# Layer 0 without a branch, with folded weights and word masks: one change to a two-layer graph attention kernel

## The chip, the cores and the metric

The kernel runs on one core of a Trainium2 chip. The metric is the time of one execution on the device in microseconds (us), median of several executions. In what follows PE is the tensor engine, PEld its weight loads, DVE the vector engine, ACT the scalar engine, POOL the GpSimd engine and SP the engine that issues most loads. The granted clock is the share of its full speed that PE was given. The chain of waits is the work that ended last, followed back step by step to what released it. A seam is a stretch between two stages in which PE has next to nothing to do. PSUM is where these kernels keep the tiles that PE writes.

## The reference, cut to what matters

There are 4096 nodes with 512 features, a dense 4096x4096 adjacency of edge weights, and 32 graphs of 128 nodes each, so that one row tile of 128 rows is one graph.

```python
# layer 0: attention inside each graph, softmax over the whole row
h = relu(layernorm(x))
q, k, v = h @ Wq.T + bq, h @ Wk.T + bk, h @ Wv.T + bv
a = where(same_graph, q @ k.T / sqrt(512), 0)
scores = (a + adj + adj) * where(same_graph, 1, -1e6)
x = x + (softmax(scores) * same_graph) @ v
# layer 1: graph attention with 8 heads of 64 columns; the term of row i cancels in its softmax
h = relu(layernorm(x))
mx = h @ W ;  t[j, head] = sum_d mx[j, head, d] * a_dst[head, d]
x = x + softmax over {j : adj[i, j] > 0} of t[j], applied to mx
```

Outside its own graph a row's scores are -2e6 times an edge weight. They are 0 for a missing edge, and so they count in the softmax's sum.

## The kernel before, where the change touches it

A flag from the group pointers decides at the start whether layer 0 runs in its tiled form. Layer 0 goes through 16 groups of two row tiles, in plain order. The buffers of x come from the same pool of three as the adjacency's.

```python
graphs_in_tiles = nc.values_load(flag_i[0:1, 0:1], min_val=0, max_val=1)
with tc.If(graphs_in_tiles > 0) as branch:
    with (tc.tile_pool(name="adj0", bufs=3) as ap, tc.tile_pool(name="sb0", bufs=2) as sb, ...):
        for g in range(NT // G):
            xg = load_x(ap, G * g, G)
            qT, kT, v = projections(sb, ps_t, ps_p, wq, wk, wv, xg)   # norm, transposes, q, k, v
            for t in range(G):
                i = G * g + t
                a = ap.tile([P, N], F32, name="a")
                nc.sync.dma_start(a, adj[ts(i, P), :])
                mask_T(ps_a, sb, a, i)        # a > 0 in bf16, 32 transposes, cast to bytes, store
                ...                           # graph-id matmul, scores, s = own block's scores
                for n, (c0, c1) in enumerate(others):
                    nc.vector.tensor_reduce(least[:, n : n + 1], a[:, c0:c1], AX.X, ALU.min)
                ...                           # nmax = -(largest score of the row)
                for n, (c0, c1) in enumerate(others):
                    nc.scalar.activation(a[:, c0:c1], a[:, c0:c1], AF.Exp, bias=nmax,
                                         scale=2.0 * NEG, accum_out=sums[:, n : n + 1])
                ...                           # exp of s, transpose, times v
                nc.vector.scalar_tensor_tensor(x1, po, rsum, xg[:, t, :], ALU.mult, ALU.add)
                nc.scalar.dma_start(x1_d[i], x1)
```

Layer 1 first prepares 32 tiles (norm, transposes, product with W, t on VectorE, exp, split in two parts) and then aggregates: for each row tile 32 x 3 matmuls of 348 columns over the transposed mask.

```python
ta = sb.tile([P, H, HD], F32, name="ta")
nc.vector.tensor_mul(ta.rearrange("p h d -> p (h d)"), pm, a_sb)
nc.vector.tensor_reduce(t, ta, AX.X, ALU.add)
```

## Time and profile before

The median is 1378.01 us in the comparison with the changed kernel (1377.6 to 1379.15, 4 runs). The stages of the profiled execution, read from the stage boundaries that the prediction shows further down:

| stage | from, to (us) | length |
|---|---|---|
| start, until layer 0's loads have landed | 0 to 30 | 30 |
| layer 0 | 30 to 712 | 682 |
| layer 1, preparation with its two seams | 712 to 878 | 166 |
| layer 1, aggregation | 878 to 1369 | 491 |
| tail | 1369 to 1378.5 | 9.5 |

To compare versions of layer 0, I use the **group spacing**: the time between the first group's last output and the last group's, divided by 15. Here it is (713.97 - 77.02)/15 = 42.5 us. In the changed order the last of the 15 is short, because the last group has no next group to prepare.

In the groups of instructions (line, engine, operation, tile, shapes, count, then busy us and mean ns of one, then the idle time before them), these two are what VectorE does to an adjacency tile besides the mask's cast:

```profile
L243 DVE TENSOR_REDUCE least<-a 128x1 f32<-128x3968 f32 (+30 forms) x62 | 138.6, 2277 | 1.8 <-DMA a<-adj 1.8
L141 DVE TENSOR_SCALAR a<-a 128x2048 bf16<-128x2048 f32 x64 | 77.3, 1221 | 6.8 <-DMA a<-adj 6.8
```

The minimum costs 138.6/32 = 4.3 us a tile.

### The profile page before, as it was taken

How to read it: one execution, taken by the hardware profiler on the slowest of the kernel's cores; microseconds unless marked ns; L12 is line 12 of the kernel's file. 1: busy time of each engine (PE TensorE's matmuls, PEld its weight loads, DVE VectorE, ACT ScalarE, POOL GpSimd, SP SyncE). 2: the span in 40 equal slices, each digit the busy share in tenths (PEclk: the TensorE clock that was granted, in tenths of full speed). 3: DMA queues.
4: the chain of work that ended last, by engine and by line, in shares of the span. 5: the costliest groups of instructions: out<-in, count | busy, mean ns of one | idle time of the engine just before them, and what ended most of it. 6: DMA issues, size and time to landing. Idle time of an engine off the chain costs nothing.

```text
span 1378.5 us, 15799 instructions
## 1 busy us (share of the span) xinstructions
PE 1189.4 (86%) x6313; PEld 961.9 (70%) x6313; DVE 642.0 (47%) x1194; ACT 463.4 (34%) x606; POOL 166.4 (12%) x264
## 2 busy tenths in 40 slices
PE   2897888897878977788848999799999999999997
PEld 1665555665556655565624444699999999999997
DVE  3856756656656566474538888121112111211121
ACT  0334544334444244433522233232223222322230
POOL 0101010100001000000004554010001000100010
PEclk9988988988889887898869999899999999999999
DMA  6245442344532344223222221212111211121110
GB/s 254 113 160 183 183 151 110 121 168 184 183 134 102 132 183 183 105 95 152 108 90 65 56 67 39 92 62 87 67 62 61 90 64 62 61 92 62 61 31 33
DMA packets 39527, 148.50 MB, mean 108 GB/s; under 512 B 4368, under 2 KB 4368, under 8 KB 35344
## 3 DMA queue, kind: packets, MB, share of 16 engines
q1 hardware_dynamic: 25616, 113.80, 23.6%
q10 hardware_dynamic: 9216, 16.78, 3.2%
q0 software_dynamic: 4608, 16.78, 3.0%
q8 instruction: 52, 0.85, 0.3%
q14 instruction: 35, 0.29, 0.1%
HBM read 113.79 MB, written 33.55 MB: 107 GB/s over the span
## 4 chain that ended last, share of the span: by engine, by line
PE 44%; DVE 5%; ACT 2%; POOL 2%; issue 1%; DMA 1%; SPq 0%; ACTq 0%; POOLq 0%; DVEq 0%
PE pg L424 36%; PE pm L388 4%; PE pp L179 2%; PE pp L190 1%; DVE e L404 1%; DVE hn L130 1%; DVE ta L390 1%; ACT parts L411 1%; POOL rstd L128 1%; PE pp L269 1%; ACT hT L134 1%; ACT a L253 1%; DMA row<-x_d 1%; POOL parts L412 0%; DVE at L150 0%
## 5 line engine op out<-in xcount | busy, mean ns | idle before, releaser
L424 PE MATMUL pg<-parts,at 128*128 128x348 f32 x3072 | 491.3, 323 | 9.1 <-ACT at L420 9.1
L424 PEld LDWEIGHTS pg<-parts,at 128*128 128x128 f32 x3072 | 491.0, 189 | 9.7 <-ACT at L420 9.7
L431 DVE TENSOR_TENSOR tot<-tot,pg 128x522 f32<-128x522 f32 x32 | 22.4, 700 | 412.4 <-ACT tot L430 412.4
L430 ACT COPY tot<-pg 128x522 f32<-128x522 f32 x32 | 19.1, 596 | 363.5 <-PE pg L424 363.5
L243 DVE TENSOR_REDUCE least<-a 128x1 f32<-128x3968 f32 (+30 forms) x62 | 138.6, 2277 | 1.8 <-DMA a<-adj 1.8
L253 ACT ACTIVATE a<-a,nmax 128x3968 f32<-128x3968 f32 (+30 forms) x62 | 123.7, 1996 | 22.3 <-DVE nmax L247 21.2
L145 PE MATMUL pa<-ident_b,a 128*128 128x128 bf16 x1024 | 88.9, 241 | 45.7 <-DVE a L141 22.8
L388 PE MATMUL pm<-w_sb,hT 128*128 128x512 f32 x256 | 116.7, 609 | 11.3 <-ACT hT L134 11.3
L179 PE MATMUL pp<-hT,wq 128*128 128x256 f32 x512 | 121.7, 399 | 5.2 <-ACT hT L134 4.8
L145 PEld LDWEIGHTS <-a 128*128 128x128 bf16 x1024 | 75.6, 109 | 63.4 <-issue 33.0
L420 ACT CAST at<-at 128x4096 fp32r<-128x4096 fp8e4 x32 | 115.9, 3621 | 5.3 <-DMA row<-x_d 4.9
L179 PEld LDWEIGHTS pp<-hT,wq 128*128 128x128 f32 x512 | 101.2, 201 | 23.2 <-ACT hT L134 9.0
L179 PE MATMUL pp<-hT,wk 128*128 128x256 f32 x512 | 113.1, 379 | 0.0
L190 PE MATMUL pp<-wv,hT 128*128 128x512 f32 x256 | 112.5, 593 | 0.0
L148 ACT ACTIVATE at<-pa 128x1024 fp8e4<-128x1024 bf16 x64 | 64.9, 1017 | 140.0 <-PE pa L145 140.0
L179 PEld LDWEIGHTS pp<-hT,wk 128*128 128x128 f32 x512 | 97.4, 190 | 13.1
L480 POOL TENSOR_TENSOR tot<-tot,row 128x512 f32<-128x512 f32 x32 | 41.3, 1290 | 462.9 <-DVE tot L447 462.9
L388 PEld LDWEIGHTS pm<-w_sb,hT 128*128 128x128 f32 x256 | 48.2, 194 | 69.9 <-issue 51.3
L193 DVE TENSOR_TENSOR v<-pp,bv_sb 128x512 f32<-128x512 f32 x32 | 22.1, 692 | 147.6 <-PE pp L190 147.6
L190 PEld LDWEIGHTS pp<-wv,hT 128*128 128x128 f32 x256 | 48.7, 190 | 54.3 <-issue 53.5
L269 PE MATMUL pp<-v,sT 128*128 128x512 f32 x64 | 64.8, 1117 | 24.7 <-ACT sT L267 24.6
L150 DVE CAST at<-pa 128x1024 fp8e4<-128x1024 bf16 x64 | 78.0, 1219 | 5.6 <-PE pa L145 4.0
(79 smaller groups left out, 958.1 us busy)
## 6 DMA issues: line engine op xcount, KB each, us to landing
a<-adj SPq DMA_DIRECT2D x32, 2048.0 KB, 9.1
at_d<-at POOLq DMA_DIRECT2D x32, 512.0 KB, 3.9
row<-x_d SPq DMA_DIRECT2D x64, 256.0 KB, 3.2
at<-at_d SPq DMA_DIRECT2D x32, 512.0 KB, 4.5
xg<-x SPq DMA_DIRECT2D x16, 512.0 KB, 7.1
x_d<-x ACTq DMA_DIRECT2D x32, 256.0 KB, 6.5
out<-tot ACTq DMA_DIRECT2D x32, 256.0 KB, 3.7
wq<-wqT SPq DMA_DIRECT2D x1, 1024.0 KB, 5.2
```

Source lines behind the costliest of these rows:

```text
L145: nc.tensor.transpose(pa[:, c, :], a01[:, ts(8 * q + c, P)], ident_b)
L148: nc.scalar.activation(dst, pa, AF.Copy, saturate=False)
L150: nc.vector.tensor_copy(dst, pa, saturate=False)
L179: nc.tensor.matmul(pp[:, : G * P], w[:, k, ts(m, P)], hT[:, k, :], start=(k == 0), stop=(k == KC - 1),)
L190: nc.tensor.matmul(pp, hT[:, k, ts(t, P)], wv[:, k, :], start=(k == 0), stop=(k == KC - 1))
L243: nc.vector.tensor_reduce(least[:, n : n + 1], a[:, c0:c1], AX.X, ALU.min)
L253: nc.scalar.activation(a[:, c0:c1], a[:, c0:c1], AF.Exp, bias=nmax, scale=2.0 * NEG, accum_out=sums[:, n : n + 1],)
L269: nc.tensor.matmul(po, sT, v[:, t, :], start=True, stop=True)
L388: nc.tensor.matmul(pm, hT[:, k, :], w_sb[:, k, :], start=(k == 0), stop=(k == KC - 1))
L420: nc.scalar.copy(at, at8)
L424: nc.tensor.matmul(pg[:, c, : 2 * CW1], at[:, j, :], parts[:, j, c].rearrange("p s w -> p (s w)"), start=(j == 0), stop=(j == NT - 1),)
L480: nc.gpsimd.tensor_add(num, num, row)
```

## The change

The intent has six parts:

- Layer 0 runs unconditionally for the case of one graph per tile. The bounds and the pointers are checked once at the end, and one branch there leads to a general path.
- q.k is formed as (h M + c).h with M = Wq.T Wk folded at the start, so that one projection takes the place of two.
- The exponentials run without the row maximum; the final check covers the range.
- Four mask bytes are packed in a 32-bit word. PE transposes 8 words per tile instead of 32 bf16 blocks.
- The next group's norm, projection and values are written among the present group's work.
- In layer 1, t comes out of PE as extra columns of the weights.

```diff
-    with tc.If(graphs_in_tiles > 0) as branch:
+    def mask_bytes(pool, a):
+        a8 = pool.tile([P, N], FP8, name="a8")
+        nc.vector.tensor_scalar(
+            a8.rearrange("p (c w b) -> p c b w", c=NW, b=BY),
+            a.rearrange("p (c b w) -> p c b w", c=NW, b=BY),
+            0.0, 1.0, ALU.is_gt, ALU.add, saturate=False,
+        )
...                                     (8 transposes of a8.bitcast(F32) per tile, two copies)
-            for g in range(NT // G):
-                xg = load_x(ap, G * g, G)
-                qT, kT, v = projections(sb, ps_t, ps_p, wq, wk, wv, xg)
+        xg[0] = load_x(sb, 0, G)
+        m_sb, c_sb, u_sb, z_sb = fold(wp, ps_t, ps_p)
...                                     (loads, and the first group's norm, values, projection)
+        for g in range(NG):
+            last = g + 1 == NG
+            if not last:
+                nhT, nr = normed(g + 1)
+            ss = []
+            for t in range(G):
+                i = G * g + t
+                a8 = mask_bytes(sb, aa[i])
+                ss.append(soften(aa[i], hT, gT, r, t, i))
+                mask_T(ps_a, sb, a8, i)
+                if i + G < NT:
+                    aa[i + G] = load_adj(ap, i + G)
+            if not last:
+                ngT = queries(nhT)
+            nvs = []
+            for t in range(G):
+                attend(ss[t], vs[t], g, t)
+                if not last:
+                    nvs.append(values(nhT, t))
+            if g + 2 < NG:
+                xg[g + 2] = load_x(sb, G * (g + 2), G)
...                                     (in soften: no minimum, no maximum, no graph-id matmul)
-        ta = sb.tile([P, H, HD], F32, name="ta")
-        nc.vector.tensor_mul(ta.rearrange("p h d -> p (h d)"), pm, a_sb)
+                pm = project1(ps_m, hT, w1x)      (2 x 260 columns: 256 of W and 4 of t)
...
+    bad = nc.values_load(bad_i[0:1, 0:1], min_val=0, max_val=1)
+    with tc.If(bad > 0):
...                                     (the general path)
```

x moved from the pool with three buffers to the pool `sb`, which has two.

## The prediction

> **What bounds the kernel now.** I first cut the execution at the stage boundaries that the chain of waits shows and read each engine's busy time per stretch. The columns are: stretch, length, busy us (instructions) of PE, weight load, DVE, ACT, POOL, then granted clock, DMA share, GB/s.
>
> ```profile
> 0.00:30.00 30.00, 3.32 (x12) 2.36 (x12) 8.80 (x16) 2.48 (x3) 2.65 (x14) 1.00 0.62 232
> 30.00:712.00 682.00, 557.84 (x2835) 403.15 (x2835) 422.01 (x693) 285.76 (x442) 53.21 (x92) 0.85 0.38 142
> 712.00:724.00 12.00, 3.05 (x7) 1.10 (x7) 2.35 (x6) 0.60 (x1) 0.79 (x2) 0.50 0.65 219
> 724.00:868.00 144.00, 133.46 (x388) 64.30 (x389) 121.81 (x255) 41.95 (x95) 67.24 (x123) 0.98 0.19 54
> 868.00:878.00 10.00, 0.88 (x4) 0.49 (x3) 0.56 (x3) 4.65 (x4) 1.23 (x1) 0.70 0.63 209
> 878.00:1369.00 491.00, 490.82 (x3072) 490.54 (x3071) 83.80 (x217) 127.51 (x63) 40.02 (x31) 1.00 0.20 64
> ```
>
> The reader is to see three kinds of time. The last stage (layer 1's aggregation, 491 us) has PE busy all the time at full clock: only fewer or shorter matmuls would move it. Layer 0 (682 us for 16 groups of two row tiles, so 42 us a group) has PE at 82% with the clock at 0.85. And 52 us (0 to 30, 712 to 724, 868 to 878) are seams where PE does next to nothing.
>
> Next I took one group of layer 0 from the chain of waits (start, us, what).
>
> ```profile
> 632.86 14.13 PE pp L179 x64
> 646.99 6.87 PE pp L190 x16
> 653.86 0.91 PE pss L230 x8
> ...
> 660.60 1.90 PE pa L145 x16
> ...
> 670.82 2.07 PE pp L269 x2
> 672.89 1.25 PE pt L133 x6
> 674.17 0.60 ACT hT L134
> 674.82 14.08 PE pp L179 x64
> ```
>
> The period is 674.82 - 632.86 = 42.0 us. 21 us of it is dense projection, the other 21 us a chain that hops between DVE, ACT and PE. What PE waits for in that half stands in the view of waits, and what it does to the clock in narrow stretches:
>
> ```profile
> PE pt L265 <- DVE s L263: 40.3, 21, 7.0
> PE pp L269 <- ACT sT L267: 24.6, 14, 3.2
> PE pa L145 <- DVE a L141: 22.8, 22, 2.3
> PE pa L145 <- DVE at L150: 20.5, 20, 1.6
> ```
> ```profile
> 640.00:647.00 7.00, 7.00 (x34) 6.18 (x33) 2.20 (x2) 1.90 (x4) 0.00 (x0) 1.00 0.00 0
> 660.00:668.00 8.00, 5.66 (x35) 3.85 (x35) 4.43 (x11) 7.24 (x9) 0.66 (x1) 0.57 0.67 233
> ```
>
> So layer 0 is bound by PE plus waiting, and the waiting costs twice: the idle time itself, and the half clock after it. The same two L269 matmuls take 2.07 us there, while L190's, of the same shape, take 6.87/16 = 0.43 us each.
>
> **What the Trainium skill says.** (1) "TensorE: Matmul & The Clock Gate", Part 1 (the HAM clock gate): PE runs at half clock until some 3.4 us of sustained work, and falls back after an idle window. The trace agrees: 1.00 in the projections, 0.57 after the waits. (2) "VectorE: DVE Perf Modes", What auto-detection actually checks: a single-source op from SBUF to SBUF handles two elements a cycle if the outermost dimensions are even, whatever the dtype. The trace agrees for plain rows: L141 turns 2048 fp32 into bf16 in 1221 ns, which is 1.7 elements per ns at the page's 0.96 GHz. Whether a byte output with step 4 keeps the mode no run here shows. (3) "Advanced Engine Details and Errata", Memory Cachelines: a line is 16 bytes and needs two hits for full speed. Step-4 bytes give four hits a line, so I expect no penalty; not shown here either.
>
> **The change part by part: PE in layer 0, per group, at full clock.** Now: q and k 14.1; v 6.9; scores 2 x 0.91 = 1.8; the graph-id matmul 0.4 (four at 0.11); 64 bf16 mask transposes at about 0.06 = 3.7 (eight take 0.61 us in the timeline, the last one's drain of 0.2 included); eight fp32 transposes of the normed rows at 0.107 = 0.9 (eight take 1.04 with the drain); two of s 0.2; attention times v 4 x 0.43 = 1.7. Sum 29.7 of the 42.0 us, so 71%.
> - Folded weights: q.k = h M h' + terms, so one projection in place of two: -7.05 us.
> - Word masks: four mask bytes are packed into one fp32 word, so 16 fp32 transposes at 0.107 = 1.7 in place of 3.7: -2.0 us.
> - The graph-id matmul goes: -0.4.
> - New sum: 29.7 - 7.05 - 2.0 - 0.4 = 20.2 us.
>
> **DVE per tile.** Out: L243, the minimum over the row (138.6 us / 32 = 4.3), both L141 (2.4), both L150 (2.4), and the mask arithmetic (L235, L157 to L161, L263, L245, two L247: 2.3). In: mask bytes over 4096 elements, 2048 cycles at two a cycle + 0.15 fixed = 2.3 (4.4 at one a cycle); hu, a two-source pass over 512 with an accumulator, 0.75 + 0.15 = 0.9; one 512-word copy out of PSUM, 0.7; one s pass, 0.29. Kept: norm 1.4, v 0.69, x1 0.75, sums 0.3. New: 7.3 a tile, 14.6 a group (18.8 in the slow mode), from 26.4 measured (422.01/16; neighbouring instructions overlap a little, so sums of durations run somewhat high).
>
> **ACT per group.** Exps 123.7/16 = 7.7 and their accumulator reads 0.7 stay. The eight L183 copies become four (-1.9), and two L148 of 1.02 per tile become one of about 0.6 (-2.9). 17.9 becomes about 13.1.
>
> **DMA per group.** 2 x 2048 + 512 + 2 x 512 + 2 x 256 KB = 6.3 MB, unchanged. At 142 GB/s now; at 25 us it needs 250, against 232 in the first stretch at a share of 0.62, so some 370 at a full share (an estimate).
>
> PE stays the largest at 20.2. The new order, which runs the next group's norm and projection between one group's scores and its attention, should fill most of the waits. Dropping the row minimum also takes away the maximum that every exp waited for. But DVE, ACT and PE still hand s around, so I don't take 100%. At the present 71% a group takes 28.5 us, at 95% 21.3; **I choose 82%, 24.6 us**.
>
> **Layer 0's ends.** The branch goes, so loads start at about 1 us in place of 11.4. But folding adds PE work: 32 transposes (3.4 to 6.8), 32 matmuls of 512 columns at 0.43 = 13.7, u 3.4, small ones about 2, after 2 MB of weights that land at about 12 us (the first loads moved at 270 GB/s: 3.5 MB from 11.4 to 24.3). Then the first projections, 13.9, partly below that. First group ready at about 48 us; its work is then in hand, so 15 full periods and a short last group of 15 us follow: 48 + 15 x 24.6 + 15 = **432 us**, against 712.
>
> **Seam.** The stage after it no longer waits for a branch's end: 3 to 4 us in place of 12.
>
> **Layer 1's preparation.** Its 32 tiles take 144 us, 4.5 each; in the steady part 4.24, of which PE 3.9. t now comes out of the matmul: 16 matmuls of 260 columns at about 0.224 (L179's 256 columns take 0.221) = 3.6 + 0.43 of transposes = 4.0 in place of 3.9. DVE loses L390, L392, L394, L397: 2.2 of 3.8 us. So PE alone bounds it, 4.1 each: **131 us**, a gain of 13.
>
> **Second seam.** Loads and cast of the first mask tile get their own buffers and parts become 32 separate tiles: 2 us in place of 10.
>
> **Aggregation.** 3072 matmuls at 160 ns, unchanged: 491. The mask cast goes from ACT (3.6 us a tile) to DVE (2.3 to 4.4), hidden either way below 15.4 us a tile. One buffer for the byte mask in place of three is enough: load 4.5 + cast 4.4 < 15.4.
>
> **Tail.** Now 9.6 us. The lone-row arithmetic goes (-1); the bounds check adds some ten small DVE ops of 0.15, a transpose and the branch, partly beside the last store's 3.7 us: 10 to 12, say 11.
>
> Sum: 432 + 4 + 131 + 2 + 491 + 11 = **1071 us**.
>
> **The rivals.** (a) The hand-over chain stays the bound: a group keeps PE at 71%, 28.5 us, so L0 = 491 and the total 1130. For it: s still goes PE, DVE, ACT, DVE, PE, ACT, PE; DVE takes work in order, so the reciprocal that waits for 4.5 us of exps can hold up the next tile's mask. Against: the page of before has DVE at 62% and lists waits that vanish. (b) DVE becomes the bound, if the byte mask runs at one element a cycle and GpSimd's small norm ops are stalled in between: 18.8 busy plus waits, 25 to 27 us, total 1080 to 1110. (c) DMA becomes the bound: 6.3 MB at the 232 GB/s of the first stretch takes 27 us, total 1107. Against: 233 GB/s at a share of 0.67 in the narrow stretch above leaves room. (d) Nearly perfect filling, 21.3 us: 1021. (e) The final check fails on these inputs and the general path runs too: then far slower. Row sums lie near the number of non-neighbours, thousands, and t is of order one, so I give it 1%.
>
> **Range and chances.** The group period carries the spread: 21.5 to 29 us is 1025 to 1138, and the ends may add 10. I take 1025 to 1135, with 1071 in the middle of the likelier half. Even rival (a) is 18% faster, so faster by 2% 0.97, within 2% 0.02, slower 0.01.
>
> **What the profile after will show.** Right: layer 0 ends near 432; a period near 24.6 with PE clock above 0.93 in layer 0; DVE mask op about 2.3 us; DVE about 60% busy; preparation near 4.1 a tile; aggregation 491. Wrong: a mask op of 4.4 us (mode), PE waiting for DVE or for the load of the adjacency rows as the longest waits, a clock still at 0.85, or an aggregation that lengthens because the cast now competes on DVE.

## More of the kernel before

In the waits of the load queue (who waited for whom, us in total, times, longest), the load of x waits for the output that frees its buffer, but not long:

```profile
SPq L88 <- DVE x L271: 66.8, 13, 6.1
```

## The result, and the profile after

The changed kernel takes 1100.02 us (1095.26 to 1101.49, 4 runs). The ratio to the kernel before is 0.7976, with a 95% interval of 0.7951 to 0.8. A ratio is the mean time of one kernel's fast runs over that of the other's of the same rounds, so it is not quite the ratio of the medians.

The stages of the changed kernel follow (stretch, length, busy us of PE, PEld, DVE, ACT, POOL with counts, granted clock, DMA share, GB/s):

```profile
0.00:57.40 57.40, 47.52 (x172) 30.86 (x173) 16.64 (x28) 12.96 (x19) 4.48 (x19) 0.94 0.49 188
57.40:144.50 87.10, 73.55 (x331) 52.50 (x328) 46.84 (x83) 45.73 (x83) 15.69 (x23) 0.92 0.72 267
144.50:444.00 299.50, 269.05 (x1117) 183.90 (x1117) 157.88 (x284) 148.52 (x260) 67.72 (x84) 0.95 0.66 236
444.00:471.30 27.30, 17.16 (x60) 12.89 (x60) 16.27 (x28) 2.52 (x6) 7.11 (x12) 0.63 0.49 164
471.30:591.00 119.70, 119.23 (x577) 99.73 (x578) 52.20 (x105) 37.23 (x88) 64.00 (x140) 1.00 0.21 60
591.00:593.00 2.00, 0.95 (x5) 0.48 (x3) 0.69 (x1) 0.18 (x1) 0.67 (x2) 1.00 0.00 0
593.00:1083.10 490.10, 490.09 (x3072) 489.80 (x3072) 120.81 (x154) 19.15 (x32) 47.04 (x63) 1.00 0.21 65
1083.10:1099.70 16.60, 0.37 (x1) 0.08 (x1) 9.32 (x28) 0.59 (x1) 3.91 (x3) 0.59 0.06 21
```

The reader is to see where the 279 us of the two profiled spans come from. Layer 0 ends at 444 instead of 712: 268 us. The preparation with its seams takes 149 us (444 to 593) instead of 166: 17 us. (By the end of the last output, 714.7 in the kernel before, it is 271 and 14 us.) The aggregation gives 1 us, and the tail takes 7 us back.

One group in steady state, from the chain of waits (start, us, what):

```profile
380.29 0.76 DVE x L373
...
381.06 4.56 DMA xg<-x
...
385.65 1.29 DVE stats L111 x2
...
389.62 1.04 PE pt L124 x4
...
392.15 7.51 PE pp L319 x32
399.66 0.86 PE pp L371 x2
400.52 3.43 PE pp L331 x8
...
405.58 0.76 DVE x L373
```

The loop closes through a load. The output of group g (L373) frees one of the two x buffers, the next load of x goes into it, and what it brings is at once the head of the next chain: norm, transposes, folded projection, attention, output. The load queue says the same:

```profile
SPq L99 <- DVE x L373: 183.2, 14, 20.6
```

These 183.2 us in 14 waits stand against 66.8 in 13 before. The adjacency's loads stand in the same queue but were not what the x load held up: they go out some 6 us after it (387.25 after 381.06), when other buffers come free. The byte mask's operation, beside L141 of before:

```profile
L130 DVE TENSOR_SCALAR a<-a 128x4096 fp8e4<-128x4096 f32 x32 | 79.2, 2475 | 15.4 <-DMA a<-adj 15.1
```

One operation of 2475 ns does what two of 1221 ns did, at the same rate per element although the bytes are written with a step of four. The 27 us after layer 0 are in the chain of waits:

```profile
447.89 6.35 DMA a_sb<-a_dst
...
456.08 6.39 PE pm L243 x16
...
462.93 2.60 DMA row<-x_d
...
466.89 2.54 PE pm L243 x8
```

First comes a broadcast load that is issued only when layer 0's space is free; then the first tiles, with a mean PE clock of 0.63 in this stretch; then a wait for a row (the fifth). After the last matmul, at 1083.1, the chain runs through the pointer check, two operations on a single partition:

```profile
1086.47 2.30 DVE cmp L484
...
1088.87 2.28 DVE ge L491
```

### The profile page after: what moved, and what is told of

Same layout as the page of the kernel before. It is cut to its first block, busy times and chain, and to the rows that moved or that the text cites. A ratio compares the mean times of both kernels' runs of the same rounds, so it can differ in the third digit from the quotient of the medians.

```text
span 1099.7 us, 13224 instructions
## 1 busy us (share of the span) xinstructions
PE 1017.9 (93%) x5329; PEld 870.2 (79%) x5329; DVE 420.6 (38%) x708; ACT 266.9 (24%) x488; POOL 210.6 (19%) x344
## 4 chain that ended last, share of the span: by engine, by line
PE 81%; DMA 8%; DVE 5%; ACT 3%; issue 1%; POOL 1%; SPq 0%; DVEq 0%; ACTq 0%; POOLq 0%
PE pg L272 45%; PE pm L243 11%; PE pp L319 9%; PE pp L331 6%; DMA xg<-x 5%; PE pt L124 3%; PE pp L371 3%; ACT junk L354 2%; DVE stats L111 2%; PE pp L199 1%; PE pss L342 1%; DMA a<-adj 1%; DVE x L373 1%; POOL rstd L117 1%; DMA w0T<-wqT 1%
## 5 line engine op out<-in xcount | busy, mean ns | idle before, releaser
L272 PE MATMUL pg<-part,at 128*128 128x348 f32 x3072 | 490.1, 322 | 1.1 <-DVE e L251 1.1
L272 PEld LDWEIGHTS pg<-part,at 128*128 128x128 f32 x3072 | 489.8, 188 | 1.5 <-DVE e L251 1.5
L265 DVE TENSOR_SCALAR at<-at 128x4096 fp32r<-128x4096 fp8e4 x32 | 73.4, 2293 | 341.5 <-PE pg L272 341.5
L243 PE MATMUL pm<-w1x,hT 128*128 128x260 f32 x512 | 121.7, 393 | 5.6 <-DVE w1x L169 5.1
L319 PE MATMUL pp<-hT,m_sb 128*128 128x256 f32 x512 | 119.3, 393 | 1.5 <-ACT hT L125 1.4
L354 ACT ACTIVATE junk<-a 128x3968 bf16<-128x3968 f32 (+30 forms) x62 | 118.0, 1903 | 0.0
L243 PEld LDWEIGHTS pm<-w1x,hT 128*128 128x128 f32 x512 | 97.0, 194 | 24.1 <-issue 7.0
L319 PEld LDWEIGHTS pp<-hT,m_sb 128*128 128x128 f32 x512 | 100.1, 199 | 18.2 <-ACT hT L125 3.6
L130 DVE TENSOR_SCALAR a<-a 128x4096 fp8e4<-128x4096 f32 x32 | 79.2, 2475 | 15.4 <-DMA a<-adj 15.1
L150 POOL DMA_DIRECT2D at_d<-at x32 | 49.1, 1536 | 85.4 <-DVE at L149 36.4
L342 PEld LDWEIGHTS pss<-hT,gT 128*128 128x128 f32 x256 | 36.5, 202 | 27.7 <-DVE s L347 16.4
L342 PE MATMUL pss<-hT,gT 128*128 128x128 f32 x256 | 41.9, 292 | 13.8 <-DVE s L347 13.5
L231 POOL TENSOR_TENSOR part<-e,part 128x522 fp32r<-128x522 f32 x32 | 39.5, 1233 | 50.4 <-ACT e L448 34.9
```

What stands on the lines that cost most here:

```text
L130: nc.vector.tensor_scalar(a8.rearrange("p (c w b) -> p c b w", c=NW, b=BY), a.rearrange("p (c b w) -> p c b w", c=NW, b=BY), 0.0, 1.0, ALU ...
L150: nc.gpsimd.dma_start(at_d[i].rearrange("p c q b -> p (c q b)"), at8)
L231: nc.gpsimd.tensor_sub(dst[:, :, 1, :], e3, dst[:, :, 0, :].bitcast(F32))
L243: nc.tensor.matmul(pm[:, g, :HX], hT[:, k, :], w1x[:, k, g, :], start=(k == 0), stop=(k == KC - 1),)
L265: nc.vector.tensor_scalar(at.rearrange("p (c b) q -> p c b q", b=BY), at8.rearrange("p c q b -> p c b q"), -1.0, None, ALU.add,)
L272: nc.tensor.matmul(pg[:, c, : 2 * CW1], at[:, j, :], part(j)[:, c].rearrange("p s w -> p (s w)"), start=(j == 0), stop=(j == NT - 1),)
```

## The experiments

**Theory.** The loop through the x load holds the groups at a spacing of 24.5 us (25.3 over the 14 full ones). Without it PE's own sum (20.2 us in the prediction) would be the bound. Each part of the change that took work out of the loop has its share of the gain. **Rivals** are that the hand-over between the engines holds the groups, and that parts of the change lie beside the critical path. Each run below names its own.

All variants change one thing in the changed kernel, if not said otherwise. They carry one patch in the general path, which never runs: a byte load there is read as 32-bit words. All results were correct. The kernel before measured 1378.14 to 1379.75 us beside them, so the batches agree to about 2 us. The changed kernel's own four times spread over 6 us (1095.26 to 1101.49), so a difference of 5 to 7 us needs the traces beside it.

### Three x buffers

```diff
-        xg = pool.tile([P, n, D], F32, name="xg")
+        xg = pool.tile([P, n, D], F32, name="xg", bufs=3)
```

> One change to the changed kernel: three buffers in place of two for the group's rows of x. Theory A (the period of layer 0 is a loop: the store of x1 frees the buffer of x, the load takes 4.5 us, then norm, transposes, folded projection and attention follow before the next x1): with the load taken out of the loop the period falls from 24.7 us by 2 to 4 us to about 21.5, PE clock in layer 0 rises to about 1.0, and the total falls by 30 to 55 us to about 1050. Theory B (PE work and the hand-over of s set the period, the load only fills a wait that is there anyway): period 24 or more, total within 10 us of 1100.

Measured: 1042.84 us (1040.94 to 1043.73), ratio 0.7564 [0.7546, 0.7582]. That is 57.2 us less, and layer 0 ends 57.3 us earlier (385.93 against 443.25). The spacing falls from 24.5 to (385.93 - 74.80)/15 = 20.7 us. Thirteen groups of this run, in the view of stretches:

```profile
94.36:373.13 278.77, 268.48 (x1219) 187.85 (x1218) 171.26 (x308) 158.79 (x286) 79.48 (x90) 1.00 0.77 285
```

PE is busy 268.48/13 = 20.65 us a group, 96% of the time, at full clock. The mean of the 14 full spacings falls from 25.3 to 21.3 us. Theory A holds and B falls: the loop through x was the bound, and PE's sum was right under it. The spacing is not even: groups of 19.3 and about 23.5 us alternate, which the last run takes up.

### Layer 1's weights early

```diff
+            if g == 3:
+                w1x = load_w1(const, wp)
...
-            w1x = load_w1(wp)
```

> One change to the changed kernel: the weights of layer 1 and their products with a_dst are loaded and formed during layer 0. Theory A (the 27 us between the last x1 and the first steady tile of layer 1 are the late load of these weights, 1.25 MB issued at 447 us, and the four products after it): the seam falls by 12 to 18 us and the total to about 1085. Theory B (the seam is the latency of x1 through memory, norm and a cold PE): it falls by less than 5 us.

Measured: 1094.49 us (1093.29 to 1096.35), ratio 0.7945 [0.7927, 0.7963], 5.5 us less. This interval touches the changed kernel's, 0.7951 to 0.8, so the times alone don't settle it. The traces do: from the end of layer 0 to the aggregation it takes 585.1 - 441.5 = 143.6 us instead of 149.0, 5.4 less. The gain lies between the two theories. Even with the weights there, the first product with W starts 10.4 us after layer 0's end, against 12.1. The weights alone were not the seam.

### Two projections

q and k are projected separately again, with the biases, in place of the folded product; nothing is folded at the start.

```diff
-        m_sb, c_sb, u_sb, z_sb = fold(wp, ps_t, ps_p)
+        wq = load_weight(wp, wqT, "wq")
+        wk = load_weight(wp, wkT, "wk")
...
+            for dst, w, b, sc in ((qT, wq, bqs, SCALE), (kT, wk, bk_sb, 1.0)):
```

> The folding alone undone: q and k are projected separately in the new order, no u, c, z. Theory A (PE work lies on the loop of each group, in full): the period rises by 7.05 us to about 31.8, 16 groups give +113, the prologue without folding gives back about 25, so total about +88: 1188. Theory B (a third of the period is slack that more PE work can fill): period 28 to 29, total +35 to +45: about 1140.

Measured: 1179.48 us (1177.54 to 1181.09), ratio 0.8561 [0.8542, 0.858], 79.5 us more. The spacing is (530.97 - 61.65)/15 = 31.3 us. The difference of 6.8 us a group (7.3 over the 14 full spacings) is close to the 7.05 us of PE that the prediction took off for the fold. Theory A holds, B falls. Since the start is 14 us shorter without the fold (first output at 61.65 against 75.81), 15 x 6.8 - 14 = 88 us are lost up to layer 0's end, and the trace shows 530.97 - 443.25 = 87.7. In the traces 12.5 us of it come back in the seam: from layer 0's end to the aggregation it takes 136.5 us instead of 149.0. The reason is a side effect of the edit. Without the fold's tiles the weights of layer 1 are loaded at 8.55 us, not at 446.92 behind layer 0. So this variant has these weights early too, and the fold in layer 0 is worth more than 79.5 us.

### The row maximum kept

```diff
+                nc.vector.tensor_reduce(low[:, n : n + 1], a[:, c0:c1], AX.X, ALU.min)
...
+            nc.vector.tensor_reduce(nmax, s, AX.X, ALU.max, negate=True)
...
+                        junk[:, c0:c1], a[:, c0:c1], AF.Exp, bias=nmax, scale=2.0 * NEG,
```

> The row minimum and the maximum put back into the new order: per tile 4.3 us of reduction on DVE and some 0.9 of small steps, and every exp waits for them. Theory A (taking DVE work and this wait away was needed for the gain): DVE goes from 13.7 to about 24 us of a group, the period rises to 28 to 30, total +50 to +85. Theory B (DVE had slack enough, 11 us a group, to take it beside PE): period under 26, total less than +20.

Measured: 1181.05 us (1180.09 to 1181.93), ratio 0.8566 [0.8548, 0.8584], 81.0 us more. The spacing is (524.38 - 79.59)/15 = 29.7 us. Eleven groups of it:

```profile
140.74:480.24 339.50, 267.78 (x1034) 183.12 (x1033) 252.58 (x414) 139.01 (x240) 46.55 (x77) 0.85 0.56 205
```

VectorE is at 252.58/339.50 = 74%, and PE's clock is down to 0.85. Theory A holds, B falls. No engine is full, so the minimum costs by standing in a chain, not by filling VectorE.

### The branch put back

```diff
+    graphs_in_tiles = nc.values_load(flag_i[0:1, 0:1], min_val=0, max_val=1)
+    with tc.If(graphs_in_tiles > 0):
```

> The changed kernel with only the branch put back: layer 0 stands again inside a branch on a flag computed at the start from the group pointers, as in the kernel before; everything else is as in the changed kernel (1100.0 us). Theory A: the branch costs what the load of the pointers, the comparison on one partition and the register load take before the first loads of layer 0 can start, some 10 us at the front, and the seam stays as it is because the weight products and the POOL parts set it, not the branch. So +8 to +16 us, 1108 to 1116; group periods unchanged near 24.5 us. Rival B: a branch region is also a wall for every engine at its end, so that the seam grows too, by another 10 to 20 us: 1120 to 1135.

Measured: 1106.85 us (1105.57 to 1109.55), ratio 0.8038 [0.8021, 0.8055], 6.8 us more. In the chain the first load, that of x, is issued at 7.55 us instead of 0.75, which is as much as the whole difference; layer 0 keeps its spacing of (444.69 - 80.78)/15 = 24.3 us. The two traces do not show the delay carried through: the first output is 5.0 us later, the end of layer 0 only 1.4, and from there to the aggregation it takes 151.8 us instead of 149.0. So the seam does grow, by 2.8 us in this pair of traces, far less than B's 10 to 20. Being free of the branch is worth about 7 us. Theory A put it a little too high; B falls.

### The program order undone

```diff
         for g in range(NG):
-            if not last:
-                nhT, nr = normed(g + 1)
+            hT, r = normed(g)
+            gT = queries(hT)
+            vs = [values(hT, t) for t in range(G)]
```

> The changed kernel with only the program order of a group undone: norm, transposes, folded projection, values, masks, softmax and output of one group are written after one another, instead of the next group's norm, projection and values being written among the present group's. Theory A: the wait of the loop is the x load behind a two-buffer tile, and the engines run far apart anyway, so the written order is worth little: within 15 us of 1100.0. Rival B: the order is what lets PE fill a group's waits with the next group's projection; without it every group shows its chain norm, transposes, projection, softmax, output, about 30 to 33 us a group instead of 24.5, so +90 to +135 us: 1190 to 1235.

Measured: 1150.43 us (1147.93 to 1155.32), ratio 0.8341 [0.8324, 0.8358], 50.4 us more. Both theories missed: A said within 15, B at least 90. The spacing is (498.02 - 66.91)/15 = 28.7 us. (The profiled run was the slowest of the four, 1155.32 us.) Up to 250 us the chain goes through adjacency loads of 9.2 to 9.3 us; after that mostly, in six groups, through the x load, and it is longer there: 10.4 to 11.3 us, against 4.4 to 4.6 in the changed kernel. So the order shortens the loop but does not open it. The traces show why the load takes longer: here the two adjacency loads of 2 MB go out just before it (299.61, landed at 312.34; x from 304.48 to 315.71), and the DMA engines are full in its first 8 us (shares of 0.96 to 1.01 after four such loads were issued). In the changed kernel the last adjacency load has landed (378.35) when the x load starts (381.06), and the share is 0.57. No run changes this by itself.

### t on VectorE again

```diff
-                pm = project1(ps_m, hT, w1x)
+                nc.vector.tensor_mul(ta.rearrange("p h d -> p (h d)"), pm, a_sb)
+                nc.vector.tensor_reduce(tt, ta, AX.X, ALU.add)
```

> The changed kernel with t formed on VectorE again in the preparation of layer 1 (multiply of 128x512 and a reduce per tile, no product columns of the weights at the seam, one 512-wide output of TensorE instead of two of 260). Theory A: PE bounds a preparation tile at 4.21 us, of which the projection's columns are most, so the narrower matmuls take 0.1 to 0.2 us a tile off and the seam loses the weight products on VectorE (about 5 us): -5 to -12 us, 1088 to 1095. Rival B: VectorE then has about 1.2 us more per tile, 3.8 to 4.6 us in all, and becomes the bound of the preparation or lengthens its chain: +5 to +20 us.

Measured: 1120.28 us (1119.17 to 1121.48), ratio 0.8127 [0.8111, 0.8143], 20.3 us more. A falls. B has the right size (just over its upper end), and of its two causes the second: VectorE isn't the bound, but the chain grows. A tile takes 5.07 us in steady state, and VectorE is busy only 3.19 us of it, PE 4.17. The order of instructions in the timeline of one tile (start, us, engine, line) shows why:

```profile
526.73 1.23 POOL L231 TENSOR_TENSOR part<-e,part 128x522 fp32r<-128x522 f32 x1 [1.26 <-ACT part L230]
...
528.23 0.57 POOL L117 TENSOR_TENSOR rstd<-ve,neghalf 128x1 f32<-128x1 f32 x1
...
528.84 0.55 DVE L118 TENSOR_SCALAR row<-row,mv,rstd 128x512 f32<-128x512 f32 x1 [1.52 <-POOL rstd L117]
529.30 0.68 DVE L461 TENSOR_REDUCE tt<-ta 128x8 f32<-128x512 f32 x1
...
530.31 0.69 DVE L466 TENSOR_TENSOR e<-pm,e 128x512 f32<-128x512 f32 x1 [0.33 <-ACT e L464]
```

VectorE takes its work in order. The sum for t (L461) stands behind the next row's norm (L118), which waits 1.52 us for POOL's rstd (L117), which stands behind POOL's part (L231), which waits for e of the tile before; and e of this tile waits for the sum. With t out of PE the sum is not in this ring, and in the changed kernel the chain there is PE alone, 3.95 us a tile at first and 4.21 in the second half. From the last output to the aggregation the trace shows 611.8 - 445.1 = 166.7 us against 149.0, so 17.8 more; the seam and the first tiles are a little shorter without the weight products. The variant keeps the changed kernel's two accumulators in PSUM. The kernel before, with three, had 4.24 us a tile and t on VectorE. So this is what t on PE is worth in the changed structure, not over the kernel before.

### bf16 masks

```diff
-                nc.tensor.transpose(pa[:, c, :], words[:, ts(half * NW // 2 + c, P)], ident)
+                    nc.tensor.transpose(pa[:, c, :], a01[half][:, ts(8 * q + c, P)], ident_b)
```

> The changed kernel with only the mask path put back to that of before: two bf16 masks, 32 bf16 transposes of 128x128 per row tile, four copies of eight blocks each with a cast to bytes, instead of one byte mask, eight transposes of 32-bit words and two copies. Theory A: PE gets about 2 us more per group and VectorE and ScalarE about 3 us more each; in a loop where one group waits for the x load of the next and PE is near 83% filled, the period grows by most of PE's addition, +1.5 to +3 us a group, +25 to +48 us in all: 1125 to 1148. Rival B: the masks lie beside the loop's chain, in PE's free 4 us a group: less than +10 us.

Measured: 1150.43 us (1145.12 to 1151.6), ratio 0.8336 [0.831, 0.8362], 50.4 us more, just beyond A's range; B falls. The spacing is (491.60 - 76.01)/15 = 27.7 us, 3.2 more. In the chain the x load took 4.5 to 7.7 us, 5.5 on average over 14 groups, instead of some 4.5. This 1 us and PE's own 2 us are close to the 3.2; that the first of them is the cause of the rest was not tested.

### The kernel before without its row maximum

```diff
-                        nc.vector.tensor_reduce(least[:, n : n + 1], a[:, c0:c1], AX.X, ALU.min)
...
-                            a[:, c0:c1], a[:, c0:c1], AF.Exp, bias=nmax, scale=2.0 * NEG,
+                            a[:, c0:c1], a[:, c0:c1], AF.Exp, scale=2.0 * NEG,
```

> The kernel before with only the row minimum and maximum taken out (two reductions of 128 rows by 4096 columns in all, one of 128 by 128 and the folding of them, per row tile; the exponentials run without a shift; right for these inputs, not for all). Theory A: VectorE's 4.4 us of minimum per tile stand in the loop of a group, between the load of a row tile of the adjacency and the softmax, so the group period of about 42.5 us falls by 5 to 8 us, 80 to 130 us in all: 1250 to 1298, the mirror image of the 81 us that putting them back into the changed kernel cost. Rival B: the loop of the kernel before is the hand-over between PE, ScalarE and VectorE in written order, in which the minimum fills a wait: less than 30 us gained, 1348 to 1378.

Measured: 1303.57 us (1301.78 to 1304.94), ratio 0.9447 [0.9427, 0.9467], 76.2 us less than its own kernel before (1379.75). The spacing falls from 42.5 to (638.71 - 78.55)/15 = 37.3 us, and PE's clock in layer 0 rises from 0.85 to 0.94. Rival B falls, and A's gain of 80 to 130 us is missed by 4 us. One part alone, done in the old kernel, gives almost what undoing it costs in the new one (81.0).

### All that was found, mended

This one has three x buffers; layer 1's weights early; the pointer check in layer 0; four of the five bound checks in the aggregation; and the first four rows of layer 1 loaded before layer 0 ends, into four buffers outside it.

```diff
+    rowp = ctx.enter_context(tc.tile_pool(name="rowp", bufs=4))
+            if g + 2 == NG:
+                early = [load_row(sb, i) for i in range(4)]
+                row = early[i] if i < len(early) else load_row(sb, i)
```

> A version meant to beat both kernels: the changed kernel with three x buffers (alone 1042.8 us), the weights of layer 1 loaded and multiplied during layer 0 (alone -5.5 us), the check of the group pointers moved into layer 0 and four of the five bound checks moved into the aggregation, and the first four x1 rows of layer 1 loaded before layer 0 ends, into buffers that stand outside layer 0. Theory A: the seam of 27 us was its chain of loads, which are now early, so 10 to 17 us fall away there and about 6 us at the tail: 1013 to 1024. Rival B: the seam is the cold PE and the POOL parts, whatever is loaded: only tail and weights gain, 1028 to 1035.

Measured: 1026.27 us (1025.7 to 1032.4, 5 runs), ratio 0.7441 [0.7426, 0.7456], 16.6 us less than with the x buffers alone. This is between the two expectations. The tail is 11.7 us instead of 16.8 with the x buffers alone. From the last output to the aggregation it takes 528.8 - 391.7 = 137.1 us instead of 147.3 there (149.0 in the changed kernel): 10 us gained, as A had it. Together the two make 15.3 of the 16.6 us. In the trace layer 0 ends 5 us later than with the x buffers alone (390.93 against 385.93), but the profiled run was the slowest of the five, 6 us over the median, so that the pointer check and the weight products cost time in layer 0 is not shown.

### Three x buffers and the row maximum

> The changed kernel with three x buffers (alone 1042.8 us) and the row minimum and maximum put back (81 us more when put back with two x buffers). Theory A: what the minimum cost with two x buffers was amplified by the loop through the x load; with that loop open VectorE's sum per group, 13.7 plus 10 us, stands beside TensorE's 20.2 and sets a period of 24 to 26 us: +40 to +75 us over 1042.8, 1083 to 1118. Rival B: the minimum stands in the chain of a tile itself, from the adjacency's load to the softmax, with or without x buffers: the same 80 us or more, 1120 to 1140.

Measured: 1103.19 us (1101.13 to 1105.5), ratio 0.8003 [0.7986, 0.8021], 60.4 us over 1042.84. Twelve groups:

```profile
103.06:403.71 300.65, 264.70 (x1129) 181.58 (x1128) 272.29 (x454) 149.22 (x260) 51.39 (x84) 0.94 0.70 255
```

Now VectorE is at 272.29/300.65 = 91%, 22.7 us of 25.05 a group. Theory A holds, B falls. With the loop open the minimum makes VectorE nearly the bound; with it closed it cost 81.0, so a quarter of that came from the loop.

### Four x buffers

This is the mended version with four buffers for x, and the pointer check in the aggregation instead of layer 0.

```diff
-        xg = pool.tile([P, n, D], F32, name="xg", bufs=3)
+        xg = pool.tile([P, n, D], F32, name="xg", bufs=4)
```

> The version with everything mended (1026.3 us), now with four x buffers instead of three, and with the check of the group pointers in the aggregation instead of layer 0 (VectorE is busy a quarter of the aggregation, and the check takes about 5 us of it). Theory A: with three buffers the x load still stands in the chain of a pair of groups (4.5 us of 43, groups of 19.3 and 23 to 25 us in turn); with four it goes out a group earlier and the period comes near TensorE's own sum of about 20.2 us: -8 to -20 us, 1006 to 1018. Rival B: what makes every second group long is the adjacency's load or ScalarE, not x: within 5 us of 1026, a little less for the pointer check.

Measured: 1016.83 us (1016.58 to 1017.45), ratio 0.7372 [0.7359, 0.7386], 9.4 us less than the version before it. Thirteen groups:

```profile
94.89:363.09 268.20, 266.01 (x1219) 187.57 (x1218) 170.25 (x311) 158.61 (x286) 71.80 (x90) 1.00 0.79 296
```

PE is busy 266.01 of 268.20 us, 99%, at full clock. The period is 20.6 us and PE's work 20.5. Layer 0 is now bound by PE alone, the preparation nearly so (133.6 us for 32 tiles), and the aggregation was already. The gain is A's. The pointer check's move was not run by itself. But the run with three x buffers alone has no check in layer 0 either, and there the last output is at 385.93 us, against 375.24 here, although the weight products now stand in layer 0. So, as far as the traces show, the gain is the fourth buffer's. The long groups, 22 to 25 us before, became 21.4 to 23.3. With three buffers alone the chain goes through an x load of 4.4 to 4.6 us once in every second group (95.1, 137.7, 180.9, 223.7, 267.1 and 309.8 us); with four it does so twice in all (96.8 and 179.2).

## Why the prediction was right, and where a term was off

The prediction was 1071 us in a range of 1025 to 1135. 1100.02 lies in it, 29 us over the point.

- **PE's sum per group, 20.2 us: right.** It can't be read in the changed kernel itself, where PE is busy 22 us a group at a clock of 0.96, but with four x buffers it is 20.5 at full clock.
- **The filling, 82%, so 24.6 us a group: right in size, not in cause, so luck.** The 14 full spacings are 25.3 us on average. The prediction expected DVE, ACT and PE handing s around. What held the period was the loop through x, which it did not name, although the diff shows x moving to a pool of two buffers. The run with three buffers settles it: nothing else was touched in layer 0 and the full spacing fell to 21.3, the number of rival (d). Of the signs that it named, the clock came as forecast (0.95), but one sign of being wrong came too: inside layer 0 PE's longest waits are for DVE (14.8 us in all for the normed rows, 13.5 for s), and on the chain the normed rows come straight after the load of x. (Two of its sums are slightly high: a period of 29 us gives 1137, not 1138, and rival (b) 1077 to 1107.)
- **The row maximum and the fold: right.** Each by itself is worth some 80 us when undone, and the maximum 76 when done alone in the old kernel.
- **VectorE: right.** The mask operation is 2.48 us, against 2.3 predicted and 4.4 for rival (b). VectorE is busy 13.4 us a group (133.87 over ten groups), against 14.6.
- **DMA: right that it isn't the bound.** With four buffers the core moved 296 GB/s in layer 0, above the 250 the prediction needed and the 232 of rival (c).
- **Layer 0's end: 432 predicted, 444 measured.** The first group's output is at 75.8 us, against 48 + 24.6 = 72.6. The first projections end at 57.4, not 48, but the output follows 18.4 us later and not 24.6. The 14 full spacings take 354.5 us, against 14 x 24.6 = 344.4: the first five, 29.0, 27.6, 26.6, 26.3 and 25.0 us, are 11.5 us more than five at 24.6. The short last one takes 12.9 against 15. In one of these groups the chain goes through an adjacency load of 10.57 us, in another through a mask store of 5.76. The prediction had one period for all full groups.
- **The seam, 4 us: wrong.** From layer 0's end to the first product with W it takes 456.1 - 444.0 = 12.1 us, and it was 9.3 before by the same marks. The prediction saw the branch's end go and did not see that the weights, their products and the first rows were still loaded behind layer 0's buffers. With the weights alone early it is 10.4 us, with weights and rows 2.9.
- **The preparation, 131 us: right in its steady part.** From 471.3 to 592.0 us 30 tiles take 4.02 us each, as predicted within 2% (4.1), and PE bounds them. The first two take 15.3 us instead of 8, with PE at a low clock and waiting for the products and a row. So it is 135.9 in all, and 133.2 with weights and rows early. VectorE also casts two mask tiles of the aggregation among these products (2.26 and 2.29 us at 459.5 and 468.4), which the prediction did not place there.
- **Second seam and aggregation: right**, 1.1 and 490.1 us, against 2 and 491.
- **The tail: 11 predicted, 16.6 measured.** The prediction counted small operations of 0.15 us. Two of the pointer check are not small, 2.30 and 2.28 us on one partition, and stand in VectorE's queue after the last matmul. With them and four of the bound checks moved, the tail was 11.5 us.
- **The branch: right.** "Loads start at about 1 us in place of 11.4" is 0.75 measured. The branch put back costs 6.8 us and not 10, but it comes back without the graph-id comparisons that stood before it.

The misses are 12 us at layer 0's end, 12 from there to the aggregation (8.1 + 4.9 - 0.9) and 5.6 in the tail, less 0.9 in the aggregation; that is the 29. The costs of the six parts undone one by one (79.5, 81.0, 6.8, 50.4, 20.3, 50.4) add to 288 us, near the gain of 278. But the run of three buffers with the maximum shows that they are not independent, so the sum proves nothing.

What stays open: what each of the loads in flight adds to the x load when the order is undone or the masks are bf16; and why with three x buffers the x load returns to the chain in every second group and not in each.

## What to carry to other kernels

When a loop is pipelined by hand, list for each tile who frees its buffer and when the next load can go: a load that starts when the last reader of the present group is done, and that the next group's first operation needs, makes a loop as long as a whole group, whatever the engines' busy shares say. After a change that takes work off the engines, look first at the load queue's waits for a release. And an engine that takes work in order can close a ring between two tiles that have nothing to do with each other: a small sum that waits behind the next tile's norm can cost more than its own time. Last, when a part is undone, look in the trace for what else moved: here, taking out the fold also loaded the next layer's weights early.

## What the Trainium skill lacked or had wrong

- "Trainium Kernel Development and Optimization", Best Practices, advises to double-buffer in order to overlap loads with compute. Here two buffers for x did not overlap the load, because the buffer is held from the norm to the group's output; three took 57.2 us off, and a fourth, with the pointer check moved, another 9.4. The page does not say how to count the buffers that a tile needs.
- "VectorE: DVE Perf Modes", What auto-detection actually checks, states its two-port rule without a word on the output's step. A byte output with a step of four kept the rate: 4096 elements in 2475 ns, against 2048 in 1221 ns for bf16 in a row.
- "TensorE: Matmul & The Clock Gate", Part 4, gives a bf16 transpose of 128x128 some 275 ns in one kernel and does not say what one costs in a dense run. Here single records of 32-bit transposes after the start are 291 to 361 ns long on average, but they overlap: eight take 0.87 us on the chain, 0.11 each, when PE is warm. The first ones of the execution, with nothing but transposes before them, took 0.24 us each (20 in 4.72 us) while the records already gave a granted clock of 1.00. That would fit its remark that transposes don't count as PE being busy in the same way, but no run here separates it from a clock that was simply still low at the start. Either way the granted clock did not show that slowness.
- No page has the ring over VectorE, ScalarE and POOL that made a preparation tile 5.07 us with no engine busy for more than 4.17 of it.
